# Layer 0 of a four-layer network on one core: which DMA queue carries its stores and its shifted loads

## The chip, the cores and the metric

The kernel runs on one core of a Trainium2 chip. The metric is the device time of one execution in microseconds, as the median of several runs; before the change it is 4029.17 us, the median of three runs (4027.53 to 4029.35). A core has five engines that work from queues of their own: PE (TensorE, matrix products), DVE (VectorE), ACT (ScalarE), POOL (GpSimd) and SP (SyncE, which here does nothing but issue DMAs). An instruction waits in its engine's queue until its semaphores have their values, and everything behind it in that queue waits too. A DMA is issued by an engine's queue, moves its data without the engine, and raises a semaphore when it has landed.

## The reference

The input x has 8 images of 256 channels and 32 x 32 pixels (N = 1024), all in float32. Four layers follow each other; the change is in layer 0, of which this is the core (`_ln` divides by the root mean square over the channels, `_bn` is a fixed scale and shift per channel):

```python
def _attention(x, ...):                      # 4 heads, key size 32, value size 64
    qkv = _bn(_conv1x1(x, qkv_w), ...)
    q, k, v = ...
    attn = softmax(einsum('bhkn,bhkm->bhnm', q, k) * 32 ** -0.5)
    out = einsum('bhdm,bhnm->bhdn', v, attn)
    pe = _bn(_dwconv3(v_img, pe_w), ...)     # 3x3 convolution per channel of v
    return _bn(_conv1x1(out + pe, proj_w), ...)

def _edffn(x, ...):
    x = _dwconv3(_conv1x1(x, pi_w), dw_w)    # 256 -> 1024 channels
    x1, x2 = split(x)                        # 512 and 512
    x = _conv1x1(gelu(x1) * x2, po_w)        # 512 -> 256
    # FFT of 8x8 patches, times fft_p, back
    ...

def _forward(x):
    x = x + gamma1 * _attention(_ln(x), ...)
    return x + gamma2 * _edffn(_ln(x), ...)
```

Layer 1 is a deformable convolution, layers 2 and 3 are attention with routed feed-forward parts.

## The kernel before, in words

The layers are Python generators (`fast0` at L1157 for layer 0, `fast1` at L1652 for layer 1), whose instructions are recorded and then put in order by a scheduler, engine by engine; the order on each engine is fixed when the program is built. Layer 0 does not hold its intermediate images in SBUF: between its parts it stores them to DRAM and loads them again. Channels lie on the 128 partitions, in KC = 2 groups.

The main stream is `attention()`: 128 steps, 16 for each image (two halves of 512 query pixels, `gq`, by 8 blocks of 128 keys, `kt`). A step makes scores on PE (L1437), exponentials on ACT (L1443), sums of them on DVE (L1394) and products with v on PE (L1401). When a half is complete, `finish()` takes reciprocals (L1420, L1421), stores the sums (L1422), projects, adds the half of x that was loaded at `kt == 4` (L1397) and stores the result into `mids[b]` (L1432). The tile x has one buffer, so its next load waits until that store has landed.

Beside it run three more streams for other images, placed by due times in `by_time`:

- `before_attention(b)`, for the image ahead: it loads x (L1316), normalises it (L1267 on ACT, `ms` on PE, L1280 on DVE), makes v (L1325), **stores v to DRAM as `vimg` (L1329, twice per image)**, makes q and k, transposes v, and then makes the 3x3 convolution of v on PE. For that it needs v in a tile `thrice`, of one buffer: the rows of 32 channels three times, shifted by one image row up, none, and down. Per image there are four batches (c by h). A batch clears the edge by a memset on POOL (L1351), **loads three shifted copies (L1355, three DMAs of 32 partitions by 4 groups by up to 512 columns)**, and after a yield runs 12 products on PE (L1367, 24 records in the trace). The memset and the loads of a batch wait until the products of the batch before have read the tile.
- `before_gates(b)` and `gates(b)`, for the image whose attention is done: they load `mids[b]` (L1493, tile `xn2`), normalise it, multiply (`pi`, L1026), convolve on DVE (L1291), and gate; **the gated product is stored to DRAM (L1535, four per image)**. The last image keeps its products in SBUF.
- `transforms(b)`, for the image before that: it loads a quarter of the gated product (`hc`, L1609) and of `mids` (`xc`, L1611), each with two buffers and one quarter ahead, multiplies (`po`), makes the patch transform (`forward`, `backward`), adds (L1479), and **stores the quarter of the layer's output (L1480)**.

Every one of these DMAs is issued from SP's queue (`nc.sync.dma_start`). Some weights are loaded from ACT's. POOL issues no DMA in layer 0; its work there is the memsets. In layers 2 and 3 POOL issues indirect DMAs (L1058, L2345).

A tile framework adds the semaphores. For DMAs it has eight for those from SP and ACT (DMAHW0 to 7) and eight for those from POOL (DMASW0 to 7); a DMA that takes one of them up again also waits until the DMA that had it before has landed.

Of the kernel before, what the change touches and what calls it, by code (L numbers as in the profile page):

```python
# [17 lines left out]
P = 128  # L18
B = 8
C = 256  # L20
# [116 lines left out]
def img(ap):  # L137
    return ap.rearrange("p (h w) -> p h w", w=IMG)
# [1018 lines left out]
def fast0(net, io):  # L1157
    tc, nc = net.tc, net.nc
# [6 lines left out]
    with ExitStack() as ctx, ExitStack() as att:  # L1165
# [15 lines left out]
        g, bb, m, v = (vec[:, i * nb : (i + 1) * nb] for i in range(4))  # L1181
# [21 lines left out]
        def bank(name):  # L1203
            return own["X"].tile([P, HF], F32, tag="X", name=name)
# [48 lines left out]
        stored = [net.dpool.tile([KC, P, N], F32, tag=f"vimg{b}", name=f"vimg{b}") for b in range(B)]  # L1253
        mids = [net.dpool.tile([P, KC, N], F32, tag=f"mid{b}", name=f"mid{b}") for b in range(B)]
        gated = [net.dpool.tile([P, 4, 4, 2, P], F32, tag=f"gated{b}", name=f"gated{b}") for b in range(B)]

        def sc(i):
            return s[:, i : i + 1]

        def sh(i):  # L1260
            return t[:, i : i + 1]

        def normed(xn, x, sq):

            squares = [sq(k) for k in range(KC)]
            for k in range(KC):
                nc.scalar.activation(squares[k], x[:, k, :], AF.Square)  # L1267
            yield
            for h in range(2):
                ps = bank("ms")  # L1270
                for k in range(KC):
                    for j in range(4):
                        nc.tensor.matmul(
                            ps[32 * j : 32 * j + 32], lhsT=net.mean64[:, :32], rhs=squares[k][:, bass.ts(h, HF)],
                            start=(k == 0), stop=(k == KC - 1),
                        )
                nc.scalar.activation(squares[0][:, bass.ts(h, HF)], ps, AF.Ln, bias=net.eps6)
            nc.scalar.activation(squares[0], squares[0], AF.Exp, scale=-0.5)
            yield
            nc.vector.tensor_tensor(xn, x, squares[0].unsqueeze(1).to_broadcast([P, KC, N]), ALU.mult)  # L1280
# [33 lines left out]
        def before_attention(b):  # L1314
            xn = aone.tile([P, KC, N], F32, tag="xn", name="xn")
            nc.sync.dma_start(out=xn, in_=io.src[b])  # L1316
            yield
            v = aone.tile([P, KC, N], F32, tag="v", name="v")
            yield from normed(xn, xn, lambda k: v[:, k, :])
            yield  # L1320
            def projected(d, w, j, norm):
                for h in range(2):
                    ps = bank("qkv")
                    net.linear_columns(ps, w, xn, bass.ts(j, P), bass.ts(h, HF))
                    nc.scalar.activation(d[:, bass.ts(h, HF)], ps, AF.Identity, scale=sc(norm), bias=sh(norm))  # L1325

            for c in range(KC):
                projected(v[:, c, :], wv, c, 2 + c)
                nc.sync.dma_start(out=stored[b][c], in_=v[:, c, :])  # L1329
                yield  # L1330
            for d, (j, name) in ((qs, (0, "q")), (ks, (1, "k"))):
                d[b] = atwo.tile([P, N], F32, tag=name, name=name)
                projected(d[b], wqk, j, j)
                yield

            va = vas[b] = atwo.tile([P, NT, KC, P], F32, tag="va", name="va")
            for t2 in range(0, NT, 2):
                ps = bank("vT")
                for i in range(2):
                    for c in range(KC):  # L1340
                        lo = i * C + c * P
                        nc.tensor.transpose(ps[:, lo : lo + P], v[:, c, bass.ts(t2 + i, P)], net.ident)
                nc.scalar.copy(va[:, t2 : t2 + 2].rearrange("p t c d -> p (t c d)"), ps)  # L1343
                yield

            o = os[b] = atwo.tile([P, KC, N], F32, tag="o", name="o")
            for c in range(KC):
                for h in range(2):

                    edge = thrice[0:32, :, :IMG] if h == 0 else thrice[64:96, :, HF - IMG :]  # L1350
                    nc.gpsimd.memset(edge, 0.0)  # L1351
                    for j in range(3):
                        n = HF * h + IMG * (j - 1)
                        lo, hi = max(0, n), min(N, n + HF)
                        nc.sync.dma_start(  # L1355
                            out=thrice[32 * j : 32 * j + 32, :, lo - n : hi - n],
                            in_=stored[b][c].rearrange("(g p) n -> p g n", g=4)[:, :, lo:hi],
                        )
                    yield
                    ps = bank("pe")  # L1360
                    for j, s_ in enumerate((0, -1, 1)):
                        for g in range(4):
                            to, fr = (
                                img(a)[:, :, max(0, -d_) : IMG - max(0, d_)]
                                for a, d_ in ((ps[32 * g : 32 * g + 32], s_), (thrice[:, g, :], -s_))
                            )
                            nc.tensor.matmul(  # L1367
                                to, lhsT=wpe[:, c, s_ + 1, g, :], rhs=fr, start=(j == 0), stop=(j == 2)
                            )
                    nc.scalar.activation(  # L1370
                        o[:, c, bass.ts(h, HF)], ps, AF.Identity, scale=sc(4 + c), bias=sh(4 + c)
                    )
                    yield
                yield

        def attention():
# [32 lines left out]
            def finish(b, gq, A, total, x):  # L1409
                cols, o = bass.ts(gq, HF), os[b]  # L1410
                av = aone.tile([P, KC, HF], F32, tag="av", name="av")
                nc.scalar.copy(av, A)
                yield
                D = bank("D")
                for h in range(NH):
                    nc.tensor.matmul(
                        D[32 * h : 32 * h + 32], lhsT=net.unit[:, :32], rhs=total[:, h, :], start=True, stop=True
                    )
                rr = aone.tile([P, HF], F32, tag="rr", name="rr")
                nc.scalar.activation(rr, D, AF.Ln)  # L1420
                nc.scalar.activation(rr, rr, AF.Exp, scale=-1.0)  # L1421
                nc.sync.dma_start(out=net.sums[8 * b + 4 * gq : 8 * b + 4 * gq + 4, :], in_=rr[0:P:32, :])  # L1422
                nc.vector.tensor_tensor(av, av, rr.unsqueeze(1).to_broadcast([P, KC, HF]), ALU.mult)
                nc.vector.tensor_tensor(o[:, :, cols], o[:, :, cols], av, ALU.add)
                yield
                yield
                for c in range(KC):
                    ps = bank("proj")
                    net.linear_columns(ps, wproj, o, bass.ts(c, P), cols)
                    nc.scalar.activation(av[:, c], ps, AF.Identity, bias=sh(6 + c))  # L1430
                nc.vector.tensor_tensor(x, x, av, ALU.add)
                nc.sync.dma_start(out=mids[b][:, :, cols], in_=x)  # L1432

            for i, (b, gq, kt) in enumerate(steps):
                ss = [psS.tile([P, 2, HF], F32, tag="S", name="s") for _ in range(2)]
# [34 lines left out]
        def backward(b, pr, u, x):  # L1470

            back = bank("back")
            for c in range(KC):
                for pc in range(2):
                    net.columns(back[:, bass.ts(2 * c + pc, P)], u[:, pc, bass.ts(c, P)], inv, start=True, stop=True)
            nc.scalar.copy(u.rearrange("p t c -> p (t c)"), back)
            for c in range(KC):
                xt = x[:, c, :].rearrange("p (h q w) -> p q h w", q=2, w=16)
                nc.vector.tensor_tensor(xt, u[:, c].rearrange("p (q h w) -> p q h w", q=2, w=16), xt, ALU.add)  # L1479
            nc.sync.dma_start(out=io.dst[b][:, :, bass.ts(pr, C)], in_=x)  # L1480

        def patches(a, pc):

# [2 lines left out]
        def paired(t, pc):  # L1486
            return t[:, :, pc, :].rearrange("p pr (r w) -> p pr r w", w=16)
# [15 lines left out]
        def gates(b, products=()):  # L1503
# [16 lines left out]
            cv, sts = {}, {}  # L1520
# [8 lines left out]
            def gate(j):  # L1529
                a = cv.pop(4 + j)  # L1530
                for pc in range(2):
                    w = paired(sts[j], pc)
                    nc.vector.tensor_tensor(w, w, patches(a, pc), ALU.mult)
                if not products:
                    nc.sync.dma_start(out=gated[b][:, j], in_=sts.pop(j))  # L1535

            def begun(*chunks):
                made = [convolved(i) for i in chunks]
# [14 lines left out]
            if products:  # L1553
# [11 lines left out]
                x = two.tile([P, KC, N], F32, tag="xn2", name="xc")  # L1565
# [1864 lines left out]
```

## Time and profile before

The profile is of one execution. A row of the profile names the source line, the engine, the operation, what is written and read (out<-in), a count, the busy time, and then the idle time of the engine ahead of the row with what ended it. A wait that a DMA ended is put down to that DMA.

| what | value |
|---|---|
| median of three runs | 4029.17 us |
| the profiled execution's own time | 4028.16 us |
| its span, first to last instruction | 4026.3 us |
| PE busy over the span | 3691.7 us (92%) |
| DVE busy over the span | 2527.2 us (63%) |
| ACT busy over the span | 2296.6 us (57%) |
| POOL busy over the span | 569.6 us (14%) |
| DMA queue of SP and ACT (q1 and q10), packets | 182948 and 3664 |
| DMA queue of POOL (q0), packets | 19440 |
| L1355 on SP, 96 issues | 302 / 422 / 2092 ns (least, median, most) |
| L1351 on POOL, 32 memsets | 194 / 196 / 198 ns |
| first and last L1367 (products of `thrice`) | 58.2 and 1022.0 us |

The numbers of an issue row (SPq) are the time in which the queue issues the DMA; its landing comes later and can be read where another instruction waits for it.

### The profile page before, as it was taken

Reading aid. Unit: us, or ns where it says so; the run is one execution under the profiler, and the core shown is the slowest. Engines: PE = TensorE matmul, PEld = TensorE weight load, DVE = VectorE, ACT = ScalarE, POOL = GpSimd, SP = SyncE. Lnnn points to the kernel's source line nnn. Section 1 sums busy time; section 2 is a strip of 40 time slices with the busy share of each in tenths; the row PEclk is TensorE's granted clock in tenths of the full one; section 3 lists DMA queues with packets and bytes.
Section 4 is the critical chain, followed back from the end, with each engine's and each line's share of the span. In section 5 each row is a group of like instructions: output and inputs, shape, how many; then the busy total and the mean of one; then the engine's idle time right before and its main releaser. Section 6 shows DMA issues by size and latency. Waiting matters only on the chain. (4 is left out here: it accounts for less than half of the span.)

```text
span 4026.3 us, 70004 instructions
## 1 busy us (share of the span) xinstructions
PE 3691.7 (92%) x28006; PEld 1696.4 (42%) x28006; DVE 2527.2 (63%) x5030; ACT 2296.6 (57%) x3106; POOL 569.6 (14%) x646
## 2 busy tenths in 40 slices
PE   8999999999888888889999978989999999998987
PEld 3222333233233444444444435663333333336986
DVE  2388888788897888842222255853365675567455
ACT  4565656655554677734333445635777666775554
POOL 0000000000000000000000012431000151044753
PEclk9999999999999988889999988999999999999998
DMA  3313223222222677720000012432320041055776
GB/s 99 118 56 110 82 82 121 92 82 92 82 80 90 220 263 266 246 77 21 22 21 21 23 61 86 146 127 78 111 97 31 34 144 46 23 156 179 227 237 213
DMA packets 206385, 439.15 MB, mean 109 GB/s; under 512 B 21849, under 2 KB 129324, under 8 KB 193380
## 3 DMA queue, kind: packets, MB, share of 16 engines
q1 hardware_dynamic: 182948, 383.02, 29.2%
q0 software_dynamic: 19440, 46.45, 3.5%
q10 hardware_dynamic: 3664, 5.11, 0.4%
q8 instruction: 224, 3.67, 0.4%
q14 instruction: 109, 0.89, 0.1%
HBM read 281.25 MB, written 160.18 MB: 110 GB/s over the span
## 5 line engine op out<-in xcount | busy, mean ns | idle before, releaser
L1291 DVE SCALAR_TENSOR_TENSOR a<-hp,w_f_vec,a 128x961 f32<-128x961 f32 x496 | 610.7, 1233 | 94.2 <-ACT a L1284 84.8
L2829 ACT ACTIVATE e<-s,five 128x1024 f32<-128x1024 f32 x512 | 542.3, 1110 | 207.1 <-PE s L2823 205.2
L2823 PE MATMUL s<-q,k 32*128 32x512 f32 x2048 | 307.4, 640 | 0.0
L2803 PE MATMUL A<-e,v 128*32 128x512 f32 x2048 | 273.6, 606 | 16.8 <-DVE o L2808 15.0
L1394 DVE TENSOR_TENSOR sum<-sum,e 128x1024 f32<-128x1024 f32 x192 | 231.9, 1219 | 83.4 <-ACT e L1443 83.4
L1443 ACT ACTIVATE e<-s 128x1024 f32<-128x1024 f32 x256 | 250.9, 1022 | 39.5 <-PE s L1437 39.4
L1026 PE MATMUL pi<-xn,w_l_wpi 128*32 128x512 f32 x2048 | 245.2, 618 | 15.9 <-ACT va L1343 8.3
L2511 DVE SCALAR_TENSOR_TENSOR junk<-mo_x,w_f_wr 128x256 f32<-128x256 f32 x512 | 250.8, 490 | 13.5
L1401 PE MATMUL A<-e,va 128*32 128x512 f32 x2048 | 248.5, 603 | 0.1
L1437 PE MATMUL s<-q,k 32*128 32x512 f32 x1024 | 184.9, 650 | 9.6 <-ACT e L1443 9.5
L1819 PE MATMUL acc<-wt,z 128*64 128x192 f32 (+4 forms) x1344 | 133.3, 338 | 52.0 <-DVE wt L1874 51.9
L3030 PE MATMUL h<-xk,w 128*128 128x128 f32 x1192 | 152.5, 283 | 20.1 <-DVE xk L3016 20.0
L1058 POOL DMA_INDIRECT res<-y,to x149 | 148.8, 999 | 111.1 <-DVE y L3054 51.9
L2999 ACT COPY w<-w_l3f_w 128x512 f32 x149 | 92.5, 625 | 125.7 <-PE h L3030 122.2
L2823 PEld LDWEIGHTS s<-q,k 32*128 32x128 f32 x2048 | 92.6, 183 | 163.1 <-issue 158.6
L3030 PEld LDWEIGHTS h<-xk,w 128*128 128x128 f32 x1192 | 149.7, 198 | 26.1 <-DVE xk L3016 22.7
L1058 POOL DMA_INDIRECT so<-xl,rows x128 | 131.2, 1025 | 172.4 <-issue 124.9
L1512 ACT ACTIVATE hp<-pi,pib 128x512 f32<-128x512 f32 x128 | 86.8, 687 | 112.2 <-PE pi L1026 111.0
L1351 POOL MEMSET thrice<- 32x128 f32 x32 | 6.3, 196 | 999.9 <-PE pe L1367 999.8
L3050 PE MATMUL y<-w_l3f_w,hid 128*128 x596 | 143.6, 384 | 2.0 <-ACT hid L3036 1.4
L1819 PEld LDWEIGHTS acc<-wt,z 128*64 128x64 f32 x1344 | 99.3, 152 | 101.6 <-DVE wt L1874 72.2
L1026 PEld LDWEIGHTS pi<-xn,w_l_wpi 128*32 128x32 f32 x2048 | 67.9, 113 | 161.9 <-issue 135.2
(416 smaller groups left out, 6879.6 us busy)
## 6 DMA issues: line engine op xcount, KB each, us to landing
row<-shifts SPq DMA_DIRECT2D x144, 512.0 KB
x<-d SPq DMA_DIRECT2D x31, 1024.0 KB
xs<-so SPq DMA_DIRECT2D x73, 260.0 KB
so<-zero SPq DMA_DIRECT2D x5, 3380.0 KB
thrice<-vimg SPq DMA_DIRECT2D x64, 256.0 KB
xl<-mox SPq DMA_DIRECT2D x64, 256.0 KB
yg<-res SPq DMA_DIRECT2D x32, 512.0 KB
gated<-st SPq DMA_DIRECT2D x28, 512.0 KB
```

Source lines behind the costliest of these rows:

```text
L1026: self.nc.tensor.matmul(ps[32 * h : 32 * h + 32], lhsT=lhsT[:, 32 * h : 32 * h + 32], rhs=rhs, **flags)
L1058: made = self.nc.gpsimd.indirect_dma_start(**args)
L1291: nc.vector.scalar_tensor_tensor(to, fr, taps(t_), to, ALU.mult, ALU.add)
L1394: nc.vector.tensor_tensor(half, half, e[j], ALU.add)
L1401: nc.tensor.matmul(state["A"][32 * h : 32 * h + 32, c, :], lhsT=vas[b][:, kt, c, 32 * h : 32 * h + 32], rhs=e[h // 2][:, h % 2, :], start= ...
L1443: nc.scalar.activation(es[i][j], ss[j], AF.Exp, scale=SCALE)
L1819: nc.tensor.matmul(acc[o, a * IMG : e * IMG], lhsT=zs[b][:, c, t, :], rhs=wt[:, c, (a - lo) * IMG : (e - lo) * IMG], start=False, stop=(t ...
L2511: nc.vector.scalar_tensor_tensor(junk, xn[:, t, :], 1.0, self.wr[:, e, :], ALU.mult, ALU.mult, accum_out=pr[:, t, e : e + 1])
L2803: nc.tensor.matmul(A[32 * h : 32 * h + 32], lhsT=vs[b][:, kt, c * P + 32 * h : c * P + 32 * h + 32], rhs=e[:, h, :], start=first, stop=last,)
L2823: nc.tensor.matmul(ss[h // 2][:, h % 2], lhsT=ks[b][32 * h : 32 * h + 32, c, bass.ts(kt, P)], rhs=qs[b][32 * h : 32 * h + 32, c, bass.ts(h ...
L2829: anchor[:] = [nc.scalar.activation(e[:, 2 * j : 2 * j + 2], ss[j], AF.Square, scale=SCALE, bias=five)]
L3030: nc.tensor.matmul(ps[:, j, m], lhsT=ws[j][:, k, bass.ts(m, P)], rhs=xk[:, j, k], start=(k == 0), stop=(k == KC - 1),)
```

## The change

Six of the DMA calls of layer 0 take another queue: the five stores (v, sums, mid, the layer's output, gated) and the loads of the shifted copies are issued by `nc.gpsimd`, which is POOL's queue. The loads of x (L1316, L1397), of mid (L1493, L1566, L1611) and of the gated products (L1609) stay on SP's. These are 16 + 16 + 16 + 32 + 28 stores and 96 loads, 204 DMAs. Nothing else differs; line numbers stay the same.

```diff
                 projected(v[:, c, :], wv, c, 2 + c)
-                nc.sync.dma_start(out=stored[b][c], in_=v[:, c, :])
+                nc.gpsimd.dma_start(out=stored[b][c], in_=v[:, c, :])
...
-                        nc.sync.dma_start(
+                        nc.gpsimd.dma_start(
                             out=thrice[32 * j : 32 * j + 32, :, lo - n : hi - n],
                             in_=stored[b][c].rearrange("(g p) n -> p g n", g=4)[:, :, lo:hi],
                         )
...
-                nc.sync.dma_start(out=net.sums[8 * b + 4 * gq : 8 * b + 4 * gq + 4, :], in_=rr[0:P:32, :])
+                nc.gpsimd.dma_start(out=net.sums[8 * b + 4 * gq : 8 * b + 4 * gq + 4, :], in_=rr[0:P:32, :])
...
-                nc.sync.dma_start(out=mids[b][:, :, cols], in_=x)
+                nc.gpsimd.dma_start(out=mids[b][:, :, cols], in_=x)
...
-            nc.sync.dma_start(out=io.dst[b][:, :, bass.ts(pr, C)], in_=x)
+            nc.gpsimd.dma_start(out=io.dst[b][:, :, bass.ts(pr, C)], in_=x)
...
                 if not products:
-                    nc.sync.dma_start(out=gated[b][:, j], in_=sts.pop(j))
+                    nc.gpsimd.dma_start(out=gated[b][:, j], in_=sts.pop(j))
```

In the built program POOL's queue then holds, image by image, the stores, memsets and shifted loads in the order in which they stood on SP's and POOL's queues before; SP's queue of layer 0 holds only loads. A load on SP that needs a store's data, or the buffer that a store reads, waits for that store's semaphore.

## The prediction

> **What bounds the kernel.** Layer 0 runs from the start to about 1350 us of the span, beside layer 1 at the end. Its busy time comes first (start:end, length, then busy us and count of PE, PEld, DVE, ACT, POOL, PE clock, DMA share, GB/s):
>
> ```profile
> 40.00:1040.00 1000.00, 939.95 (x8800) 301.03 (x8796) 763.32 (x689) 596.67 (x733) 6.08 (x31) 0.97 0.30 93
> 1040.00:1240.00 200.00, 171.25 (x1668) 57.30 (x1660) 190.08 (x188) 111.70 (x149) 6.01 (x6) 0.91 0.27 93
> ```
>
> PE works 940 of 1000 us and the DMA engines are three tenths busy: layer 0 is bound by PE's order of work, and a DMA costs time only where PE (or ACT just ahead of it) stands waiting for it. POOL has 6 us of work. Next, the waits of layer 0 (us in total, times, longest), those that a DMA ended:
>
> ```profile
> PE pe L1367 <- DMA thrice<-vimg: 22.4, 7, 4.4
> ...
> PE po L1026 <- DMA hc<-gated: 13.0, 5, 4.3
> ...
> ACT sq L1267 <- DMA xn<-mid: 9.2, 5, 4.3
> ```
>
> With one more of 5.2 us (PEld po) this is 50 us: the most that any reordering of these DMAs can win. The waits of SP's own queue tell why some loads are late; SP stands before stores that are not ready, and loads stand behind them:
>
> ```profile
> SPq L1535 <- DVE st L1533: 328.1, 27, 21.5
> SPq L1480 <- DVE xc L1479: 189.6, 22, 19.2
> SPq L1432 <- DVE x L1431: 172.8, 16, 20.6
> ```
>
> **What moves.** 204 DMAs go from SP's queue to POOL's: 16 stores of v, 96 loads of `thrice`, 16 of the sums, 16 of mid, 32 of the result, 28 of gated. The built order of both kernels shows PE's and DVE's work unchanged but for a few neighbours (ACT swaps a square with its neighbour once per image, three groups change places where layer 1 begins): these I cost at nothing, their operations are the same and stand within a few us. On POOL the stores, the memsets of the edges (L1351) and the loads stand in the order they had on SP. So a moved DMA waits behind a subset of what it waited behind before; what is new is (a) that the loads left on SP no longer stand between them, (b) that the memset, and its wait for PE, stands in the same queue ahead of the loads, (c) what POOL needs to issue a DMA.
>
> **The price of an issue on POOL, p.** No plain DMA on POOL is in this trace. SP needs 0.34 to 0.57 us for one (v 0.34, `thrice` 0.42, mid and result 0.56: medians of the rows). POOL's nearest rows are the indirect DMAs of layer 2, 128 rows each:
>
> ```profile
> 2394.14 0.98 POOL L1058 DMA_INDIRECT so<-xn,idx  x1 [0.31 <-issue]
> 2395.42 0.97 POOL L1058 DMA_INDIRECT so<-xn,idx  x1 [0.30 <-issue]
> 2396.70 0.97 POOL L1058 DMA_INDIRECT so<-xn,idx  x1 [0.30 <-issue]
> ```
>
> 0.97 us busy and 1.28 from start to start. [...] I take p = 1.1 (and 0.1 between two), nearest to these rows. Bounds: 0.42, SP's own row, since nothing here excludes it; 2.0, about twice the indirect row, since mid and the result are 256 runs each. The rest of a landing I leave as it was: SP's first packets start about 0.5 us after the issue ends, those of the indirect rows about 0.57 us after theirs, and 128 KB have landed 1.3 us after.
>
> [...]
>
> **The sum.** I kept all computation at its times in the trace, put the moved DMAs in POOL's order (start = last of: the DMA before it issued, the tile written, the DMA it depends on landed), and compared each landing with the time at which PE or ACT arrives.
>
> *Images 0 and 1.* Here nothing blocks SP; the loads go out when PE leaves the `thrice` tile and land just in time. For one of them (SP, POOL and PE rows):
>
> ```profile
> 80.59 1.25 SPq L1355 DMA_DIRECT2D thrice<-vimg  x3
> ```
> ```profile
> 80.64 0.20 POOL L1351 MEMSET thrice<- 32x128 f32 x1 [9.64 <-PE pe L1367]
> ```
> ```profile
> 87.56 2.73 PE L1367 MATMUL pe<-thrice,w_f_wpe 128*32 128x512 f32 x24
> ```
>
> SP's third issue ends at 81.84, the last piece lands 4.5 us later at 86.4, and PE, which arrives at 87.56, does not wait. On POOL: memset to 80.85, three issues of 1.1 with 0.1 ahead of each to 84.4, landing 4.5 later at 88.9: with 0.1 for the semaphore a stall of 1.5. The six batches with as little room (of the eight in images 0 and 1) get 0.9, 1.3, 1.5, 2.4, 1.2 and 2.0: **+9.3**.
>
> *Images 2 to 7, last batch.* This is the 22.4 us row. One of the six:
>
> ```profile
> 384.58 0.57 SPq L1432 DMA_DIRECT2D mid<-x  x1
> 385.25 0.56 SPq L1480 DMA_DIRECT2D d<-xc  x1
> 388.67 0.40 SPq L1397 DMA_DIRECT2D x<-in_x_dram  x1
> 389.31 0.57 SPq L1611 DMA_DIRECT2D xc<-mid  x1
> 390.05 1.42 SPq L1355 DMA_DIRECT2D thrice<-vimg  x3
> ```
> ```profile
> 397.26 4.24 PE L1367 MATMUL pe<-thrice,w_f_wpe 128*32 128x512 f32 x24 [3.23 <-DMA thrice<-vimg]
> ```
>
> The load of x waits 3 us for the mid store to land (it overwrites the tile being stored), and `thrice` stands behind it though its tile was free at 386.6. On POOL: mid from 384.6, result to 386.9, memset to 387.2, three issues to 390.7, against 391.47 now. Landing 0.7 earlier. So the gain of 3 us in the queue is nearly all eaten by three issues at 1.1 in place of 0.42 and two stores ahead. The six images give 0.0, -0.7, -0.1, 0.0, -0.9 and +0.1: **-1.6**.
>
> *hc, once per image, six times.* SP issues it when the last gated store has landed; the store is now issued by POOL in 1.1 instead of 0.34, of which 0.1 is won back: **+0.7 x 6 = +4.1**. *xn after mid (L1493), six stalls of ACT ahead of PE:* 1.1 in place of 0.56: **+0.6 x 6 = +3.6**.
>
> Sum: 9.3 - 1.6 + 4.1 + 3.6 = 15.4, say **+16**. PE carries such stalls to its end: it is 94% busy and in order. I cost at nothing: the result and sums stores (nobody waits for them within layer 0 but a buffer two quarters later, whose loads show no stall; without that cover up to 1 us for each of 28); the memsets of layer 1 (POOL, 1200.9 to 1206.9), which now stand ahead of the last mid store, 1.7 us, covered by ACT's table load before its square; the row loads of layer 1, which leave SP earlier at 1323 (the trace has 5.9 us of ACT waits for them, so at most -6).
>
> The profiled execution took 4028.16 us (span 4026.3), 1.0 under the median of the three, 4029.17. With 16 more: 4044 for such an execution, **4045 as a median**.
>
> By the same sum p = 0.42 gives about -20 (the last batches win 2.4 to 3.4 each, nothing else loses); p = 0.85 breaks even; p = 1.28 gives +28; 1.1 with 1.6 for the 256-run stores +26; 1.8 gives +62 and 2.0 +77, as then all 20 batches with under 8 us of room stall.
>
> **Rivals.** *Faster, 4008 to 4021 (15%).* POOL issues a plain DMA as SP does, below 0.7 us. For: SP's 0.42 row is also a plain DMA, and 3 us of queueing per image really go. Against: all 405 DMAs that POOL issues here take 0.95 us or more. It decides at p = 0.85, at the `thrice` batch that ends each image; at 0.5 the time is about 4013. *No change, 4021 to 4037 (17%).* p of 0.7 to 0.95, or landings 0.3 us shorter after POOL's issue (the 128 KB rows hint at it; -7 at p = 1.1). *Much slower, above 4060 (20%).* [...] *The forecast, 4037 to 4060 (48%).*
>
> [...]
>
> The change may also not do what it says: loads stay on SP, but those of hc, xn, x and xc wait for stores on POOL, so each chain store-landing-load crosses two queues and keeps its length. That is in the sum.
>
> **Range and chances.** The range takes the faster rival and most of the dear one: 4008 (p = 0.42) to 4095 (p = 1.8 and a little), leaving some 1 in 10 above and a few in a hundred below. Within 0.2% (8 us) is what a measurement here cannot tell from no change. Faster by more 0.15, within 0.17, slower 0.68.
>
> **What would show it.** Right: POOL rows of plain DMAs of 1.0 to 1.3 us; waits of PE pe for `thrice` of about 30 us in 13 pieces, six of them before 165 us; hc and xn waits up 0.6 each; `thrice` issues of the last batches starting right behind the memset. Wrong: POOL rows under 0.7 or near 2; a clock different from 0.97 in the 40 to 1040 stretch; differences outside layer 0.

## The result, and the profile after

The changed kernel takes 4039.27 us (median of 20 runs, 4022.52 to 4045.09), the kernel before, run beside it, 4025.69 us (20 runs, 4017.11 to 4037.22). The ratio is 1.0029, with a 95% interval of 1.0019 to 1.0040: about 12 us slower (8 to 16). The ratios here and below are estimated from the runs themselves and need not be the quotient of the two medians (1.0034 here); differences in us are worked out from the ratios. The forecast was 4045, "slower" the likeliest sign. The time is near the forecast; the reason that was given for it is not what happened, and most of what follows is about that.

The profiled execution after has a span of 4034.0 us, 7.7 over the one before. The two stretches of layer 0 look as they did (columns as before: length, then busy us and count of PE, PEld, DVE, ACT, POOL, PE clock, DMA share, GB/s):

```profile
40.00:1040.00 1000.00, 934.08 (x8712) 298.48 (x8708) 757.74 (x682) 590.78 (x726) 107.61 (x207) 0.97 0.30 93
1040.00:1240.00 200.00, 167.17 (x1672) 55.39 (x1668) 187.45 (x186) 113.47 (x151) 18.09 (x25) 0.92 0.26 91
```

POOL has 107.6 us of work in place of 6.1, PE 5.9 us less in the same 1000: it stands more. The first sum of layer 1 (DVE L1870) starts at 1359.0 instead of 1349.8, so in this execution 9.2 us are lost in layer 0; the rest of the span is within 1.5 us of what it was. Next, the groups of POOL (busy us, mean ns of one, then the idle time ahead and what ended it):

```profile
L1355 POOL DMA_DIRECT2D thrice<-vimg x96 | 53.4, 562 | 31.4 <-DMA vimg<-v 26.3 <-POOL thrice L1351 4.8
L1432 POOL DMA_DIRECT2D mid<-x x16 | 11.1, 691 | 183.4 <-DVE x L1431 174.0 <-issue 9.4
```

POOL issues a `thrice` load in 0.56 us and a mid store in 0.69, not in the forecast's 1.1. And the waits that a DMA ended (us, times, longest):

```profile
PE po L1026 <- DMA hc<-gated: 24.8, 5, 5.5
...
PE pe L1367 <- DMA thrice<-vimg: 12.7, 7, 3.6
...
PE po L1026 <- issue: 6.4, 1, 6.4
```

The waits for `thrice` fell from 22.4 to 12.7. Those for hc rose from 13.0 to 31.2: the row that ends with "issue" belongs to them, as hc landed at 361.76 there and PE went on at 361.85. A wait is not the whole price. The groups of these two products, over the first 1350 us of the kernel before:

```profile
L1026 PE MATMUL po<-w_l_wpo,hc 128*32 128x256 f32 x1792 | 105.6, 387 | 14.3 <-DMA hc<-gated 13.0 <-ACT rr L1421 1.3
L1367 PE MATMUL pe<-thrice,w_f_wpe 128*32 128x496 f32 (+1 forms) x768 | 96.7, 640 | 22.4 <-DMA thrice<-vimg 22.4
```

and of the changed one:

```profile
L1026 PE MATMUL po<-w_l_wpo,hc 128*32 128x256 f32 x1792 | 115.0, 413 | 31.3 <-DMA hc<-gated 24.8 <-issue 6.4
L1367 PE MATMUL pe<-thrice,w_f_wpe 128*32 128x496 f32 (+1 forms) x768 | 89.4, 599 | 12.7 <-DMA thrice<-vimg 12.7
```

The same products take 9.4 us longer when they had to wait for hc, and 7.3 less when they no longer wait for `thrice`. Busy and wait added up, `po` went from 119.9 to 146.3 (+26.4), `pe` from 119.1 to 102.1 (-17.0), both together from 239.0 to 248.4. These 9.4 us match the 9.2 that layer 0 lost. So the change wins 17 us at one place and loses 26 at another.

Why products become longer is seen in the clock that PE was granted. The stretch 359 to 364 of the kernel before, with a `po` that had waited 2.02 us, and 360 to 368 of the changed one, after 6.45 us:

```profile
359.00:364.00 5.00, 4.29 (x72) 2.86 (x76) 4.89 (x5) 0.58 (x2) 0.00 (x0) 1.00 1.00 238
```
```profile
360.00:368.00 8.00, 6.15 (x64) 3.33 (x68) 5.51 (x5) 0.00 (x0) 0.00 (x0) 0.57 0.28 87
```

The granted clock is 1.00 in the first stretch and 0.57 in the second, and the same 64 products take 6.50 us in place of 3.66. The records of the granted clock show 0.50 in stretches: in the first 1350 us of the kernel before there are 20, each 3.41, 6.83 or 10.24 us long, in the changed one 20 of 3.41 or 6.83. In the kernel before one of them reaches into the products behind each of the 12 waits of PE of 3.2 us or more between 200 and 1350 us. No fixed length of wait decides: after 3.09 us of waiting (image 7, before) 24 products took their usual 2.73 us, after 2.41 us (image 7 of E2, below) 4.43.

Now the place itself, image 3. SP's queue before:

```profile
353.16 0.34 SPq L1535 DMA_DIRECT2D gated<-st  x1
355.87 1.25 SPq L1609 DMA_DIRECT2D hc<-gated  x2
357.22 1.52 SPq L1355 DMA_DIRECT2D thrice<-vimg  x3
```

POOL's and SP's queues after:

```profile
351.13 0.54 POOL L1535 DMA_DIRECT2D gated<-st  x1 [19.26 <-DVE st L1533]
351.71 0.20 POOL L1351 MEMSET thrice<- 32x128 f32 x1
352.24 1.68 POOL L1355 DMA_DIRECT2D thrice<-vimg  x3 [0.33 <-POOL thrice L1351]
```
```profile
354.14 1.20 SPq L1609 DMA_DIRECT2D hc<-gated  x2
```

Before, the second `thrice` batch of an image was issued behind the two hc loads, because SP stood there until the gated store had landed. On POOL nothing holds it: its three loads, some 750 KB, go out 1.9 us ahead of hc (two loads of 512 KB). PE needs hc first, at once, and this `thrice` batch only some 9 us later. By the landings in the trace, counted from the end of the issue, the first hc came after 3.12 us before and after 7.09 us in the changed kernel; the third `thrice` piece came after 6.50 us, while the third batch of an image, which has little beside it, needs 4.0 to 4.3. Both are slowed. From 354.7 to 358.9 us the packets of POOL's queue took 71.8% of the time of the 16 DMA engines and those of SP's 28.7%, so the two share them. The same holds in images 4 to 7: the first hc lands 6.0 to 7.7 us after the gated store in these five images, 3.7 to 4.2 before.

### The profile page after: what moved, and what is told of

It reads as the page before. It is cut to its first block, busy times and chain, and to the rows that moved or that the text cites. A ratio compares the mean times of both kernels' runs of the same rounds, so it can differ in the third digit from the quotient of the medians.

```text
span 4034.0 us, 70068 instructions
## 1 busy us (share of the span) xinstructions
PE 3683.6 (91%) x28006; PEld 1692.8 (42%) x28006; DVE 2527.0 (63%) x5030; ACT 2298.3 (57%) x3106; POOL 692.8 (17%) x850
## 5 line engine op out<-in xcount | busy, mean ns | idle before, releaser
L3030 PEld LDWEIGHTS h<-xk,w 128*128 128x128 f32 x1192 | 149.2, 198 | 29.9 <-DVE xk L3016 25.6
L1026 PE MATMUL po<-w_l_wpo,hc 128*32 128x256 f32 x1792 | 115.0, 413 | 31.3 <-DMA hc<-gated 24.8
L2137 POOL TENSOR_TENSOR x<-x,yn 128x1024 f32<-128x1024 f32 x16 | 37.3, 2351 | 573.0 <-ACT yn L2136 324.7
```

What stands on the lines that cost most here:

```text
L1026: self.nc.tensor.matmul(ps[32 * h : 32 * h + 32], lhsT=lhsT[:, 32 * h : 32 * h + 32], rhs=rhs, **flags)
L3030: nc.tensor.matmul(ps[:, j, m], lhsT=ws[j][:, k, bass.ts(m, P)], rhs=xk[:, j, k], start=(k == 0), stop=(k == KC - 1),)
```

## The experiments

Theory O (overtaking) is the one just told. Rival C says that the moved stores are the loss, as a load on SP waits for each gated and mid store; rival Q that SP's loads suffer from any DMA of POOL, whatever its size. The experiments ran on three chips, of which one is slower as a whole (before: 4099.87 us, the others 4027.26 and 4025.90); each ratio is to the kernel before on the same chip.

### One batch alone, and the change without it

E1: the kernel before, with

```diff
-                        nc.sync.dma_start(
+                        (nc.gpsimd if (c, h) == (0, 1) else nc.sync).dma_start(
                             out=thrice[32 * j : 32 * j + 32, :, lo - n : hi - n],
```

> The kernel before, with only the three loads of each image's second thrice batch (c = 0, h = 1) on POOL; every store and all other loads stay on SP. Theory O (overtaking): these loads used to be issued behind the two hc loads on SP; from POOL they go out about 2 us ahead of them and put 768 KB in front of data that PE needs first, so PE waits longer for hc in images 3 to 7, about 2.5 to 4 us each, and its clock drops after so long a wait, about 1.5 us more each. It expects 15 to 26 us over the kernel before, waits of PE po for hc of 22 us or more in place of 13. Theory C (crossing): what costs is the chain of a store on POOL and the load on SP that waits for it (gated to hc, mid to xn), with POOL's dearer issue. No store is moved here, so it expects -4 to +4 us and hc waits of 13 us.

Measured: 4122.81 us, ratio 1.0066 (1.0053 to 1.0079), +27 us. The waits of PE for hc:

```profile
PE po L1026 <- DMA hc<-gated: 29.5, 6, 5.4
```

24 of the 204 DMAs, and no store among them, lose about twice what the whole change loses, a little over what O expected (the medians alone say +23). O holds; C cannot give this. A long head start is not needed: in image 6 only the first of the three loads went out ahead of hc, by 0.27 us, the others 0.28 and 0.82 us behind it, and PE still waited 4.77 us. Behind hc on SP's own queue, in the kernel before, the same three loads left hc its landing at 3.7 to 4.2 us behind the gated store.

E2: the changed kernel with the same batch back on SP (`nc.sync if (c, h) == (0, 1) else nc.gpsimd`).

> The changed kernel, with only the three loads of each image's second thrice batch back on SP, behind the hc loads. Theory O: the hc waits fall back to about 13 us, PE stays at its full clock there, and what the change wins at the last batch of each image remains: 4 to 15 us under the kernel before, so 16 to 27 under the changed one. Theory C: all stores are still on POOL, so it stays at +8 to +14 over the kernel before, with hc waits of 20 us or more.

Measured: 4093.01 us, ratio 0.9987 (0.9974 to 0.9999), -5 us, hc waits 18.6. As O expected, the loss turns into a gain by putting back three loads per image; but the gain is at the low end of what O expected, and hc waits stay 5 us over those of before, so the stores cost something too.

### Bytes or queue

E6: the changed kernel, the second batch with one of four groups only.

```diff
-                            out=thrice[32 * j : 32 * j + 32, :, lo - n : hi - n],
-                            in_=stored[b][c].rearrange("(g p) n -> p g n", g=4)[:, :, lo:hi],
+                            out=thrice[32 * j : 32 * j + 32, : 1 if (c, h) == (0, 1) else 4, lo - n : hi - n],
+                            in_=stored[b][c].rearrange("(g p) n -> p g n", g=4)[:, : 1 if (c, h) == (0, 1) else 4, lo:hi],
```

> The changed kernel, whose second thrice batch of each image loads one of its four groups of 32 channels only (the other three quarters of that tile keep old data: this part of the computation is left out). The three DMAs are still issued by POOL at the same places, ahead of hc, but carry 192 KB in place of 768. Theory O (bytes ahead of hc): hc lands 2.5 to 3 us sooner, hc waits fall from 25 to 31 us to 12 to 17, and the kernel is 15 to 25 us faster than the changed one, so 4 to 13 under the kernel before. Theory Q (it is not the bytes but POOL's queue: three DMAs of POOL under way hold up SP's loads whatever their size): hc waits stay at 22 or more and the time at +8 to +14 over the kernel before.

Measured: 4021.41 us, ratio 0.9981 (0.9971 to 0.9991), -8 us. hc waits 16.1, and 2.6 in one row of "issue":

```profile
L1026 PE MATMUL po<-w_l_wpo,hc 128*32 128x256 f32 x1792 | 107.5, 392 | 18.7 <-DMA hc<-gated 16.1 <-issue 2.6
```

The first hc of image 3 lands 3.26 us after the end of its issue, and in images 3 to 7 it lands 3.6 to 4.3 us after the gated store (before the change 3.7 to 4.2). The DMAs are as many, from the same queue, ahead of hc as in the changed kernel (only in the first 235 us, where no hc is loaded yet, do some groups of PE stand in another order); with a quarter of the bytes the loss is gone. Q falls: it is the bytes of `thrice` in flight. The waits are a little over O's 12 to 17; what is left of them, 18.7, is what the gated stores on POOL give by themselves (18.0 in E9 below).

E7: the changed kernel with hc on POOL too (`nc.gpsimd.dma_start(out=hc, ...)`), so that hc stands ahead of `thrice` in one queue again.

> The changed kernel, with the hc loads (L1609) on POOL's queue too. In its built order they stand behind the gated store and ahead of the second batch's thrice loads, as they stood on SP before. Theory O: the order hc before thrice is back, so hc waits are 12 to 18 us and the time is 3 to 12 us under the kernel before. Theory Q: POOL's queue is the slow one, so hc itself becomes slow; waits of 25 us or more, +10 us or more over the kernel before.

Measured: 4028.61 us, ratio 1.0008 (0.9995 to 1.0021), +3 us (-2 to 8); hc waits 19.2 and one of 3.3. Under the changed kernel by some 8 us, but short of O's -3 to -12. The trace shows why the order alone does not bring all back: from the landing of the gated store to the start of the hc issue POOL takes 0.55 to 0.66 us, SP 0.02 to 0.14 (E5), and the issue takes 0.77 us, SP 0.6. The first hc lands 4.4 to 5.1 us after the gated store; on SP with nothing ahead 3.7 to 4.1, in the changed kernel 6.0 to 7.7 in these five images.

### Where the gain is

E3: the kernel before, with only the last batch on POOL (`(c, h) == (1, 1)`).

> The kernel before, with only the three loads of each image's last thrice batch (c = 1, h = 1) on POOL. They then no longer stand behind the load of x that waits for the mid store. Both theories expect a gain here, from the measured POOL issue of 0.56 us: 2 to 3 us less waiting in each of six images and no drop of PE's clock there: 8 to 17 us under the kernel before, with PE pe waits for thrice of under 12 us in place of 22.4. If the loads of this batch too get in front of something, it is 0 to -5.

Measured: 4084.72 us, ratio 0.9962 (0.9948 to 0.9976), -16 us (-21 to -10), as expected; `thrice` waits 14.0, a little over what was expected, and the group's busy time 91.8 instead of 96.7.

E12: all batches but the second on POOL, all stores on SP.

> The kernel before, with the first, third and last thrice batches of each image on POOL, the second on SP, all stores on SP. The last batch alone gave -16 us (interval -21 to -10). If the first and third have room, as their rows show (nothing urgent is in flight beside them), this is -10 to -20 us, with hc waits of 12 to 15. If they too get in front of something, 0 to -8.

Measured: 4004.45 us, ratio 0.9944 (0.9926 to 0.9963), -22 us (-30 to -15), a little more than expected, and the fastest kernel of this study. Its two groups:

```profile
L1026 PE MATMUL po<-w_l_wpo,hc 128*32 128x256 f32 x1792 | 106.1, 389 | 14.4 <-DMA hc<-gated 14.4
L1367 PE MATMUL pe<-thrice,w_f_wpe 128*32 128x496 f32 (+1 forms) x768 | 87.0, 585 | 6.2 <-DMA thrice<-vimg 6.1
```

`po` is what it was before (119.9, now 120.5), `pe` 25.9 us less: the gain that was looked for in SP's queue, without the loss.

### What the stores cost

E4: all stores on POOL, all loads on SP.

> All stores on POOL, all loads, the thrice loads among them, on SP. Theory O: thrice stands behind hc again, so hc waits are about 13 us, with 0.2 us for each store that POOL issues more slowly: 0 to +5 us. The last batch is still behind the load of x that waits for mid, so nothing is won there. Theory C: the stores bring the whole loss of the change and the loads on POOL its gain, so +12 to +25 us, hc waits of 20 us or more.

Measured: 4109.34 us, ratio 1.0030 (1.0015 to 1.0046), +12 us (6 to 19); hc waits 16.3, `thrice` 22.6. The time is C's, the waits are nearly O's (the profiled execution took 4102.06, 7 us under the median). So I split the stores.

E8: only the gated and the mid stores on POOL.

> The kernel before, with only the gated and the mid stores on POOL, the two whose landing a load waits for. The stores alone (all five kinds) cost 12 us with an interval of 6 to 19. Theory C in the size that the profile gives (0.21 us more per gated store, 0.13 per mid store, six times each, and PE's half clock after some of the longer waits): +2 to +8 us. If instead POOL's in-order queue is what costs (a store behind another store that is not ready), these two alone, with nothing else on POOL but memsets, cost -2 to +3 us, and the rest lies with the v, sums and result stores.

Measured: 4042.35 us, ratio 1.0041 (1.0026 to 1.0057), +16 us, above what either reading expected; hc waits 17.0, `thrice` 29.9. So I took them one by one.

E9: only the gated stores.

> The kernel before, with only the gated stores on POOL. The order of PE, DVE and ACT is the one of before. If the loss of the two chain stores (+16 us, 10 to 23) is the chain gated store to hc, this alone costs +5 us or more. By the profile (0.2 us more of issue, hc waits 0.3 longer, five or six times) it costs 0 to +5, with hc waits of 13 to 15 us.

Measured: ratio 1.0012 (1.0000 to 1.0024), +5 us (0 to 10). hc waits 18.0, `po` 110.5 busy. The time lies on the border of the two expectations, the waits above both. From issue to landing a gated store takes 2.62 us on SP and 2.90 on POOL. Six times 0.28 us are 1.7; the group's waits grew by 4.3 over E5's 13.7 (12.2 for hc, and one of 1.4 that ACT ended just after hc had landed) and the products behind them by 4.6. Of the latter, two waits of 2.51 us that were followed by half clock make 3.4:

```profile
518.65 5.35 PE L1026 MATMUL po<-w_l_wpo,hc 128*32 128x256 f32 x64 [2.51 <-DMA hc<-gated]
```

At full clock these 64 products take 3.66 us. What adds the rest is not settled.

E10: only the mid stores.

> The kernel before, with only the mid stores on POOL. Here the built order of SP's queue also changes: ahead of the last thrice batch the load of xc (which waits for the result store) now stands ahead of the load of x, instead of behind it. If this is where the loss of the two chain stores lies, +8 to +18 us and thrice waits of 27 us or more in place of 22. If it is the gated store, 0 to +4 and thrice waits of 21 to 24.

Measured: ratio 1.0029 (1.0016 to 1.0043), +12 us (6 to 17), `thrice` waits 28.9: what was expected if the loss lies in the order on SP. E5 is the kernel before once more, for profiles to set beside these:

> The kernel before, unchanged, for a profile on the same chip as the kernels beside it. Every theory expects the profile shown of it: hc waits of PE of about 13 us, thrice waits of about 22 us, the first sum of layer 1 (DVE L1870) at about 1350 us. Another chip may change what comes after.

Measured: 4024.33 us, hc waits 12.2, `thrice` 22.7, first sum of layer 1 at 1348.8. SP's queue ahead of the last `thrice` batch of image 3, in E5 and then in E10:

```profile
384.12 1.74 SPq L1480 DMA_DIRECT2D d<-xc  x1
387.46 0.40 SPq L1397 DMA_DIRECT2D x<-in_x_dram  x1
388.08 0.57 SPq L1611 DMA_DIRECT2D xc<-mid  x1
388.83 1.42 SPq L1355 DMA_DIRECT2D thrice<-vimg  x3
```
```profile
388.60 0.58 SPq L1480 DMA_DIRECT2D d<-xc  x1
393.04 0.54 SPq L1611 DMA_DIRECT2D xc<-mid  x1
393.62 0.60 SPq L1397 DMA_DIRECT2D x<-in_x_dram  x1
394.38 1.29 SPq L1355 DMA_DIRECT2D thrice<-vimg  x3
```

The built order has put the load of xc ahead of the load of x. xc takes a tile that the result store still reads, and is issued when that store has landed (at 388.07 in E5, 393.02 in E10). In E5 x had gone out 0.6 us earlier, behind the landing of mid; in E10 it too stands behind the result's landing, and `thrice` starts 5.8 us after the result's issue began, in E5 4.7. In E4 the mid store is on POOL as well, but x is still ahead of xc, and the `thrice` waits are 22.6, as before; as E4 moves the other stores too, this points to the order, and not to the mid store's own issue, without proving it. One call moved, and the scheduler turned two others around.

E11: only the v, sums and result stores.

> The kernel before, with only the v, sums and result stores on POOL. The prediction costed them at nothing within layer 0. It stands if this is -4 to +4 us. The difference between all stores (+12) and the two chain stores (+16) says -4 with some 9 of uncertainty, so a gain of up to 8 us is open: the result store would no longer hold up the loads behind it on SP.

Measured: ratio 1.0011 (1.0000 to 1.0023), +4 us (0 to 9), at the edge of what was expected; there is no gain. hc waits 13.8, `thrice` 23.0, as before; the interval just touches no change, and no place in the trace was found for these us.

### The parts beside the whole

| what is on POOL | us to before, interval | `po` busy+wait | `pe` busy+wait |
|---|---|---|---|
| nothing (before; E5) | 0 | 119.9; 119.6 | 119.1; 119.5 |
| all (the change) | +12, 8 to 16 | 146.3 | 102.1 |
| second batch (E1) | +27, 22 to 32 | 146.6 | 120.3 |
| all but second batch (E2) | -5, -11 to 0 | 126.8 | 106.3 |
| last batch (E3) | -16, -21 to -10 | 120.1 | 105.8 |
| first, third, last batch (E12) | -22, -30 to -15 | 120.5 | 93.2 |
| all stores (E4) | +12, 6 to 19 | 124.0 | 121.5 |
| gated (E9) | +5, 0 to 10 | 128.5 | 122.3 |
| gated and mid (E8) | +16, 10 to 23 | 124.6 | 127.6 |
| mid (E10) | +12, 6 to 17 | 122.8 | 128.5 |
| v, sums, result (E11) | +4, 0 to 9 | 120.1 | 122.4 |

The stores one by one sum to 5 + 12 + 4 = +21, all together (E4) they cost +12: the mid stores alone come with the turned order on SP, which neither E4 nor the changed kernel has. With E4 for the stores the parts sum to +27 - 22 + 12 = +17, the whole gives +12; the intervals together allow some 12 either way, so the parts account for the whole within the noise.

## Why the time was right and the reason not

*What bounds the kernel: right, but not complete.* In the profiled execution all of the loss lies in layer 0, at waits of PE for DMAs and the products behind them. "The most that any reordering can win" was put at 50 us, from waits alone; the products behind a wait cost as well. In E12 the waits of `pe` fell by 16.2 us and its busy time by 9.7.

*The price p = 1.1: wrong.* No run shows it: the medians on POOL are 0.56 for `thrice` (128 runs), v and gated, and 0.69 for mid (256 runs). The indirect rows were the wrong neighbours, and the forecast's lower bound, SP's own row, was the near one. The landing behind the issue is as on SP (gated 2.29 and 2.36 us, mid 2.53 and 2.47, medians). From issue to landing a gated store takes 0.28 us longer on POOL and a mid store 0.06, where the forecast had 0.7 and 0.6.

*Images 0 and 1, +9.3: did not come.* One wait of 0.73 us became one of 1.71. Of the announced 13 waits of about 30 us there were 7 of 12.7 us.

*Last batch, -1.6: mis-sized.* Right in kind, but -17.0 in size for all `thrice` batches together (the last batch alone, E3: -13.3): waits 9.7 less, as the three issues take 1.68 us and not 3.5, and busy time 7.3 less, as the products less often run at half clock (89 of the 768 took more than 0.87 us before and 24 after, with a median of 0.58), which the step did not count.

*hc, +4.1: the step that failed.* The forecast said that "a moved DMA waits behind a subset of what it waited behind before" and saw in it only what the moved DMA wins. The loads that stood behind hc also left hc alone; "that the loads left on SP no longer stand between them" was listed as new under (a), and no price was put on it, since "the rest of a landing I leave as it was". Measured: +26.4, of which E1 shows that the second batch makes nearly all (146.6 alone, 146.3 in the whole). The part that was forecast, the dearer gated issue, is there and smaller: 0.28 us in place of 0.7 per store.

*xn after mid, +3.6: not shown.* From the issue of mid to its landing is 0.06 us more, not 0.6. The waits of ACT for xn rose from 9.2 to 14.5 us, but they are 8.6 in E1, 10.4 in E12 and 12.7 in E11, where mid stays on SP; what moves them is not settled.

*Costed at nothing: nearly.* The v, sums and result stores cost 0 to 9 us.

*The rivals.* The premise of "faster" (p under 0.7) came true, and its own sum gives about -13 at 0.56 (on a line between -20 at 0.42 and 0 at 0.85). The kernel is slower all the same, by a mechanism that no rival had. By the forecast's own list of signs, POOL rows under 0.7 were to show it wrong. The dear rival (above 4060) did not come: no plain DMA of layer 0 held POOL longer than 0.79 us. Two errors, 1.1 for 0.56 and no price for the overtaking, cancelled; that the time came out near the forecast is luck.

## What to carry to other kernels

A queue that makes a load wait may be keeping it out of the way of a more urgent one: before moving it, list for each moved transfer what is issued within the next few us from other queues, how many bytes would go ahead of it or beside it, and who needs them first. Move the transfers one group at a time; here a part of the change is worth -22 us and another +27. Price a wait of several us with the slow products that follow it, and read the built order again even on queues that a change only takes from.

## What the runs showed of the hardware

- In the changed kernel a `thrice` load (128 runs) holds POOL's queue 0.55 to 0.61 us, a mid or result store (256 runs) 0.67 to 0.79; the 405 indirect DMAs of the kernel before have a median of 0.98. SP's medians for the moved ones are 0.34 to 0.56.
- In E7 POOL began the hc issue 0.55 to 0.66 us after the landing that it waited for; in the changed kernel it began a `thrice` load 0.28 to 0.30 us after the landing of v, and SP the hc issue 0.02 to 0.15 us after that of the gated store.
- In images 3 to 7 of the changed kernel hc and a `thrice` batch of some 750 KB, begun 1.0 to 2.3 us earlier from the other queue, were in flight together and shared the DMA engines (in image 3 71.8% and 28.7% of their time, `thrice` the former, from 354.7 to 358.9 us): hc landed 6.0 to 7.7 us behind the gated store, before the change 3.7 to 4.2.
- The granted clock of PE falls to 0.50 in stretches of one to three times 3.41 us: 20 in the first 1350 us before (106 us in all), 20 after (96 us). From 200 to 1000 us its means over 200 us are 0.95 to 0.98 before and 0.97 to 1.00 in E12. Whether a wait of 2.4 to 3.4 us is followed by such a stretch differs from place to place: after 2.41 us in E2 and 3.23 us before (397 us) the 24 products took 4.43 and 4.24 us, after 3.09 us before (1020 us) 2.73.
